# Expert layers on gathered token slots instead of all tokens, with indirect row fetches, in a hybrid attention / mixture-of-experts kernel

## The chip, the cores and the metric

One core of a Trainium2 chip runs one program. It has five engines with queues of their own: TensorE (PE, with its weight loads listed apart as PEld), VectorE (DVE), ScalarE (ACT), GpSimd (POOL) and SyncE (SP), which here only starts transfers. Each engine works through its instructions in order and waits on semaphores for the others. The metric is device time in microseconds (us) of one execution, the median of several runs. All data are fp32.

## The reference, cut to what matters

Eight sequences of 512 tokens with 128 channels go through four residual layers, each on the layernormed input: causal attention, a mixture of experts, an RWKV block, and the same mixture of experts again.

```
x = embeddings                                    # [8, 512, 128]
x = x + attn(layernorm(x))                        # one head of 128 channels
x = x + ffn(layernorm(x))
x = x + rwkv(layernorm(x))                        # itself residual, with a scan over the tokens
x = x + ffn(layernorm(x))

ffn(x):  scores = softmax(x @ Wg)                 # 32 experts
         weights, indices = top_k(scores, 4)
         y[t] = sum over the 4 chosen e of weight * ((silu(x[t] @ W1[e]) * (x[t] @ W3[e])) @ W2[e])
         # hidden size 64; an expert takes at most 2048 of the 4096 tokens
         return y + (silu(x @ Ws1) * (x @ Ws3)) @ Ws2    # shared expert, hidden size 128
```

A token uses 4 of 32 experts, so of a sequence's 512 tokens an expert gets 64 on average.

## The kernel before

The tokens of one sequence are held as four tiles of 128 (token-major: 128 tokens on the partitions) or turned by TensorE into channel-major tiles of 128 channels by 512 tokens. An fp32 product of 128x128 weights with 512 columns shows in the profile as two MATMUL records and two LDWEIGHTS records.

The eight sequences pass through the four layers one behind the other, as a pipeline. Step `s` of the loop at the end of the function `tile_block_kernel` holds attention of sequence `s`, the first expert layer of `s-1`, the RWKV block of `s-2` and the second expert layer of `s-3`; there are 11 steps, and steps 3 to 7 hold all four. Inside a step, `interleave` traces the experts of one layer side by side with attention, and then those of the other layer side by side with RWKV. The tracing order and a scheduler in the language give each engine one fixed order of instructions.

`norm` takes statistics on DVE (L143, L145), the inverse square root on POOL (`rstd`, L146 and L147) and applies it on DVE (L149). `turn` transposes on TensorE (L157).

`route` follows attention and RWKV: scores on TensorE (L173), softmax and the four largest on DVE (L175 to L194), a running count of earlier tokens per expert (POOL, L201, and TensorE, L205 and L206) for the capacity, and the resulting gates, turned, written to DRAM, and read back by `load_gates` with each expert's row spread over 64 partitions (tile `g`, 64 copies).

`experts` works densely: all 16 pairs of experts (two of 64 hidden units fill 128 partitions) on all 512 tokens, plus the shared expert. For each pair: `a` (L251) and `c` (L253) on TensorE, `tanh` on ACT (L257), `h = (tanh + 1) a` on DVE (L258), `v = c * gate` on DVE (L263), `h * v` on POOL (L264), and the product `y` (L239), which accumulates over the pairs in PSUM. At the end `y` is copied (L270), turned and added to the input (L273).

Of the kernel before, what the change touches and what calls it, by code (L numbers as in the profile page):

```python
# [15 lines left out]
P = 128          # partitions, tokens of a tile, channels  # L16
B = 8            # sequences
S = 512          # tokens of a sequence
NJ = S // P      # token tiles of a sequence
E = 32           # experts  # L20
NP = E // 2      # expert pairs: two experts of 64 hidden units fill 128 partitions
NQ = NP // 4     # gate loads of a sequence, each for four pairs
TOPK = 4
CAP = 4 * (B * S * TOPK) // E   # tokens that one expert takes at most
# [3 lines left out]
# Columns of the packed [128, .] weights.  # L28
# [9 lines left out]
# Columns of the packed per-channel vectors.  # L38
# [4 lines left out]
def interleave(heavy, light):  # L43
    """Traces two streams of work side by side: two steps of the light one behind each of the heavy one."""
    for _ in heavy:
        for _ in range(2):
            next(light, None)
    for _ in light:
        pass
# [3 lines left out]
def kernel(ctx: ExitStack, tc: tile.TileContext, x, small, vecs, w13, w2, out):  # L53
    nc = tc.nc

    const = ctx.enter_context(tc.tile_pool(name="const", bufs=1))
    xin = ctx.enter_context(tc.tile_pool(name="xin", bufs=3))
    wk2 = ctx.enter_context(tc.tile_pool(name="wk2", bufs=2))
    wk1 = ctx.enter_context(tc.tile_pool(name="wk1", bufs=1))
    mo = ctx.enter_context(tc.tile_pool(name="mo", bufs=3))  # L60
    gates = ctx.enter_context(tc.tile_pool(name="gates", bufs=2))
    st = ctx.enter_context(tc.tile_pool(name="st", bufs=3))
    dram = ctx.enter_context(tc.tile_pool(name="dram", bufs=2, space=bass.MemoryType.DRAM))
    ps_m = ctx.enter_context(tc.tile_pool(name="ps_m", bufs=2, space=PSUM))
    ps_y = ctx.enter_context(tc.tile_pool(name="ps_y", bufs=1, space=PSUM))
    ps_l = ctx.enter_context(tc.tile_pool(name="ps_l", bufs=3, space=PSUM))

# [1 line left out]
    x0 = {}  # L69

    def load_x(b):
        if b < B:
            x0[b] = xin.tile([P, NJ, P], F32, tag="x0", name=f"x0_{b}")
            nc.sync.dma_start(out=x0[b], in_=x[b].rearrange("(j p) d -> p j d", p=P))

    load_x(0)
    sm = const.tile([P, NCOLS], F32, tag="sm", name="sm")
    cut = _COLS["Wg"][0]
    nc.sync.dma_start(out=sm[:, :cut], in_=small[:, :cut])
    vec = const.tile([P, len(_VECS)], F32, tag="vec", name="vec")  # L80
    nc.scalar.dma_start(out=vec, in_=vecs)
    nc.sync.dma_start(out=sm[:, cut:], in_=small[:, cut:])
    w13s = const.tile([P, NP, 2, P], F32, tag="w13", name="w13s")
    w2s = const.tile([P, NP, P], F32, tag="w2", name="w2s")
    for q in range(NQ):
        nc.sync.dma_start(out=w13s[:, 4 * q : 4 * q + 4], in_=w13[:, 4 * q : 4 * q + 4])
        nc.sync.dma_start(out=w2s[:, 4 * q : 4 * q + 4], in_=w2[:, 4 * q : 4 * q + 4])
    load_x(1)
# [5 lines left out]
    def V(name):  # L94
        i = _VECS.index(name)
        return vec[:, i : i + 1]

# [7 lines left out]
    tri = const.tile([P, P], F32, tag="tri", name="tri")     # tri[i, t] = i <= t  # L105
# [5 lines left out]
    wdec = const.tile([P, 1], F32, tag="wdec", name="wdec")  # -exp(time_decay)  # L111
    nc.scalar.activation(wdec, V("time_decay"), AF.Exp)
    nc.vector.tensor_scalar(wdec, wdec, -1.0, None, ALU.mult)

    # Scores and the values looked for in them, each behind or before four marks that every row
    # has: the match below then finds just the four largest, the first of equals first.
    sc, lst, tot = [], [], []
    for f in range(2):
        s = const.tile([P, NJ, E + 4], F32, tag=f"sc{f}", name=f"sc{f}")
        m = const.tile([P, NJ, 8], F32, tag=f"lst{f}", name=f"lst{f}")  # L120
        for i in range(4):
            nc.gpsimd.memset(s[:, :, E + i : E + i + 1], -1.0 - i)
            nc.gpsimd.memset(m[:, :, 4 + i : 5 + i], -1.0 - i)
        t = wk2.tile([P, NJ + 1, E], F32, tag=f"tot{f}", name=f"tot{f}_start")
        nc.gpsimd.memset(t[:, NJ, :], 0.0)
        sc.append(s)
        lst.append(m)
        tot.append(t)

    def light(name):  # L130
        return ps_l.tile([P, S], F32, tag="l", name=name)

    def flat(t):
        return t.rearrange("p j d -> p (j d)")

# [1 line left out]
    def norm(src, dst, name):  # L137
        """dst = (src - mean) / sqrt(var + eps) over the channels of [128 tokens, 4, 128]."""
        stats = st.tile([P, NJ, 6], F32, tag="stats", name=f"stats_{name}")
        mv = st.tile([P, NJ, 2], F32, tag="mv", name=f"mv_{name}")  # L140
        rstd = st.tile([P, NJ], F32, tag="rstd", name=f"rstd_{name}")
        for j in range(NJ):
            nc.vector.bn_stats(out=stats[:, j, :], in_=src[:, j, :])  # L143
        for j in range(NJ):
            nc.vector.bn_aggr(out=mv[:, j, :], in_=stats[:, j, :])  # L145
        nc.gpsimd.tensor_scalar(rstd, mv[:, :, 1], EPS, None, ALU.add)  # L146
        nc.gpsimd.tensor_tensor(rstd, rstd, nhalf, ALU.pow)  # L147
        for j in range(NJ):
            nc.vector.tensor_scalar(  # L149
                dst[:, j, :], src[:, j, :], mv[:, j, 0:1], rstd[:, j : j + 1], ALU.subtract, ALU.mult  # L150
            )

    def turn(src, name):
        """[128 tokens, 4, 128 channels] -> PSUM [128 channels, 512 tokens], or back."""
        p = light(f"turn_{name}")
        for j in range(NJ):
            nc.tensor.transpose(p[:, j * P : (j + 1) * P], src[:, j * P : (j + 1) * P], ident)  # L157
        return p

    def route(xa, f, b):  # L160
        """Layernorm, scores, the top four experts, capacity; gates go out over the partitions of
        their experts. Gates carry the factor 1/2 of silu(a) = a (1 + tanh(a/2)) / 2."""
# [34 lines left out]
        # tot[j] counts, per place in a tile, the tokens of earlier tiles that chose an expert.  # L197
# [22 lines left out]
        def load_gates(q):  # L220
            """The gates of four pairs, each over the 64 partitions of its expert."""
            t = gates.tile([P, 4, S], F32, tag="g0" if q == 0 else "g", name=f"g_{n}_{q}")
            for h in range(2):
                nc.sync.dma_start(out=t[64 * h : 64 * h + 64], in_=gv[h, q].partition_broadcast(64))
            return t
# [4 lines left out]
    def experts(f, b, xa, put):  # L230
        """xa + the shared expert + the gated experts, all of them on all tokens; put(result)."""
# [9 lines left out]
        for i in range(NP + 1):  # L241
# [8 lines left out]
            a = ps_m.tile([P, S], F32, tag="a", name=f"a_{k}")  # L250
            nc.tensor.matmul(a, wa, xT, start=True, stop=True)  # L251
            c = ps_m.tile([P, S], F32, tag="c", name=f"c_{k}")
# [16 lines left out]
        ys = mo.tile([P, S], F32, tag="ys", name=f"ys_{n}", bufs=2)  # L269
# [63 lines left out]
    def shifted(p, w, bias, name):  # L333
        """Channel-major h from PSUM, behind a column of zeros; and h - (h one token back)."""
        h = wk1.tile([P, S + 1], F32, tag="hT", name=f"hT_{name}")
        nc.gpsimd.memset(h[:, 0:1], 0.0)
        nc.scalar.activation(h[:, 1:], p, AF.Identity, bias=V(bias), scale=V(w))
        d = wk1.tile([P, S], F32, tag="dT", name=f"dT_{name}")
        nc.gpsimd.tensor_tensor(d, h[:, 1:], h[:, :S], ALU.subtract)
        return h, d  # L340

    def mixed(h, d, tm, name):
        """h * tm + (h one token back) * (1 - tm)."""
        t = wk2.tile([P, S], F32, tag="mix", name=f"mix_{tm}_{name}")
        nc.vector.scalar_tensor_tensor(t, d, V(tm), h[:, :S], ALU.mult, ALU.add)  # L345
        return t
# [4 lines left out]
    def rwkv(b):  # L351
# [22 lines left out]
        # pp_t = max(pp_{t-1} + w, k_t); pp, aa and bb start one column early with their initial state.  # L374
# [69 lines left out]
        for c in range(4):  # L444
            p = light(f"kk_{b}_{c}")
            nc.tensor.matmul(p, W("WkeyT", c * P, (c + 1) * P), xk, start=True, stop=True)  # L446
            t = wk1.tile([P, S], F32, tag="kk", name=f"kk_{b}_{c}s", bufs=4)
# [28 lines left out]
    nothing = iter(())  # L476
    for s in range(B + 3):
        a, r = s, s - 2
        m1, m2 = s - 1, s - 3
        interleave(  # L480
            experts(0, m1, x1.pop(m1), lambda t: x2.__setitem__(m1, t)) if 0 <= m1 < B else nothing,
            attention(a) if a < B else nothing,
        )
        interleave(
            experts(1, m2, x3.pop(m2), store(m2)) if 0 <= m2 < B else nothing,
            rwkv(r) if 0 <= r < B else nothing,
        )
# [41 lines left out]
```

## Time and profile before

| | |
|---|---|
| three runs | 1129.38, 1132.04, 1137.63 us; median 1132.04 us |
| profiled execution: span, first to last instruction | 1130.8 us, 9602 instructions |
| mean granted TensorE clock | 0.970 |
| TensorE busy | 988.6 us (87%) |
| DVE busy | 746.7 us (66%) |
| POOL busy | 565.0 us (50%) |
| ACT busy | 311.6 us (28%) |
| moved by DMA | 77.38 MB, of which `g` 128 x 512 KB |

The page gives no other time for the profiled execution than its span; the span lies 1.2 us below the median of the runs, so little lies around it. A row of the table of groups reads: line, engine, operation, output<-input by the program's names, shapes, count, then busy time and the mean of one instruction, then the idle time of that engine just ahead of these instructions and what ended it. "Busy" of TensorE counts overlapped instructions once, so the time that one matmul takes in a stream is read from the distance of starts in the timeline and not from its duration.

### The profile page before, as it was taken

Reading aid. Unit: us, or ns where it says so; the run is one execution under the profiler, and the core shown is the slowest. Engines: PE = TensorE matmul, PEld = TensorE weight load, DVE = VectorE, ACT = ScalarE, POOL = GpSimd, SP = SyncE. Lnnn points to the kernel's source line nnn. Section 1 sums busy time; section 2 is a strip of 40 time slices with the busy share of each in tenths; the row PEclk is TensorE's granted clock in tenths of the full one; section 3 lists DMA queues with packets and bytes.
Section 4 is the critical chain, followed back from the end, with each engine's and each line's share of the span. In section 5 each row is a group of like instructions: output and inputs, shape, how many; then the busy total and the mean of one; then the engine's idle time right before and its main releaser. Section 6 shows DMA issues by size and latency. Waiting matters only on the chain.

```text
span 1130.8 us, 9602 instructions
## 1 busy us (share of the span) xinstructions
PE 988.6 (87%) x2800; PEld 457.6 (40%) x2800; DVE 746.7 (66%) x1809; ACT 311.6 (28%) x578; POOL 565.0 (50%) x613
## 2 busy tenths in 40 slices
PE   4798988799789987998889988899889998888988
PEld 2443543344334433454334543344334443333433
DVE  2456577766866767667776678567685649588543
ACT  2231323223323332232322323232222223231221
POOL 1134345643663457534674347544484547548433
PEclk8799999999999999999999999999999999999999
DMA  5053325105332241133313240331402340142051
GB/s 184 13 118 73 81 50 112 37 13 111 78 73 50 65 96 38 45 79 80 71 38 98 59 101 17 75 86 38 114 26 50 86 112 0 38 96 65 1 123 46
DMA packets 45668, 77.38 MB, mean 68 GB/s; under 512 B 2864, under 2 KB 11184, under 8 KB 45488
## 3 DMA queue, kind: packets, MB, share of 16 engines
q1 hardware_dynamic: 45472, 76.77, 29.1%
q8 instruction: 22, 0.36, 0.1%
q14 instruction: 30, 0.25, 0.1%
q10 hardware_dynamic: 144, 0.01, 0.0%
HBM read 73.62 MB, written 3.15 MB: 68 GB/s over the span
## 4 chain that ended last, share of the span: by engine, by line
PE 47%; DVE 30%; POOL 15%; issue 4%; DMA 2%; ACT 2%; SPq 0%; POOLq 0%; DVEq 0%; ACTq 0%
PE y L239 11%; PE a L251 10%; PE c L253 10%; DVE v L263 5%; POOL h L264 4%; DVE h L258 4%; PE kk L446 3%; PE kv L459 2%; DVE wden L416 2%; PE o L325 2%; PE s L307 2%; DVE xn L149 1%; POOL rstd_f L147 1%; POOL tot L201 1%; DVE sc L184 1%
## 5 line engine op out<-in xcount | busy, mean ns | idle before, releaser
L264 POOL TENSOR_TENSOR h<-h,v 128x512 f32<-128x512 f32 x256 | 336.7, 1316 | 374.4 <-DVE v L263 299.8
L257 ACT ACTIVATE h<-a 128x512 f32<-128x512 f32 x272 | 161.5, 596 | 497.2 <-PE a L251 462.1
L251 PE MATMUL a<-fT,w13s 128*128 128x512 f32 x512 | 270.5, 612 | 11.7 <-DVE h L258 11.4
L239 PE MATMUL y<-h,w2s 128*128 128x512 f32 x512 | 265.0, 604 | 17.5 <-POOL h L264 17.5
L253 PE MATMUL c<-fT,w13s 128*128 128x512 f32 x512 | 269.3, 608 | 5.1 <-DVE v L263 5.1
L258 DVE SCALAR_TENSOR_TENSOR h<-h,a 128x512 f32<-128x512 f32 x272 | 184.7, 679 | 130.5 <-ACT h L257 129.6
L263 DVE TENSOR_TENSOR v<-c,g 128x512 f32<-128x512 f32 x256 | 174.2, 682 | 28.8 <-PE c L253 26.5
L239 PEld LDWEIGHTS y<-h,w2s 128*128 128x128 f32 x512 | 94.7, 195 | 132.0 <-issue 87.4
L253 PEld LDWEIGHTS c<-fT,w13s 128*128 128x128 f32 x512 | 96.7, 196 | 114.0 <-issue 86.9
L251 PEld LDWEIGHTS a<-fT,w13s 128*128 128x128 f32 x512 | 93.4, 196 | 107.6 <-issue 72.3
L146 POOL TENSOR_SCALAR rstd_f<-mv_f 128x4 f32<-128x4 f32 x16 | 3.6, 228 | 78.4 <-DVE mv_f L145 78.4
L149 DVE TENSOR_SCALAR xn<-x,mv_f,rstd_f 128x128 f32<-128x128 f32 x64 | 23.5, 429 | 25.5 <-POOL rstd_f L147 25.5
L446 PE MATMUL kk<-mix_ffn_tmk_c,sm 128*128 128x512 f32 x64 | 29.5, 601 | 4.8 <-DVE mix_ffn_tmk_c L345 4.8
L157 PE MATMUL turn_f<-ident,xn 128*128 128x128 f32 x64 | 16.7, 330 | 18.9 <-DVE xn L149 18.9
L325 PEld LDWEIGHTS o<-vs,prTs 128*128 128x128 f32 x160 | 23.4, 209 | 20.1 <-ACT prTs L320 18.9
L328 DVE SCALAR_TENSOR_TENSOR x<-o,aden,x 128x128 f32<-128x128 f32 x32 | 11.2, 350 | 28.5 <-PE o L325 28.4
L325 PE MATMUL o<-vs,prTs 128*128 128x128 f32 x160 | 27.4, 307 | 2.7 <-ACT prTs L320 2.7
L461 DVE SCALAR_TENSOR_TENSOR num_c<-thr_c,kv 128x512 f32<-128x512 f32 x8 | 5.5, 687 | 34.8 <-PE kv L459 34.8
L416 DVE RECIPROCAL wden<-wden 128x128 f32<-128x128 f32 x32 | 27.9, 913 | 0.0
L314 ACT ACTIVATE pr<-s,abig 128x128 f32<-128x128 f32 (+3 forms) x32 | 16.8, 524 | 36.3 <-DVE abig L311 26.9
L201 POOL TENSOR_TENSOR tot<-tot,chosen 128x32 f32<-128x32 f32 x64 | 16.9, 265 | 16.5 <-DVE chosen L194 13.3
L307 PE MATMUL s<-WKT,WQT 128*128 128x128 f32 (+3 forms) x64 | 25.0, 474 | 0.0
(173 smaller groups left out, 1169.1 us busy)
## 6 DMA issues: line engine op xcount, KB each, us to landing
g<-gd SPq DMA_DIRECT2D x128, 512.0 KB, 6.6
x<-in_x_dram SPq DMA_DIRECT2D x8, 256.0 KB, 4.2
w13s<-in_w_dram SPq DMA_DIRECT2D x4, 512.0 KB, 10.9
out_dram<-xo SPq DMA_DIRECT2D x8, 256.0 KB, 2.2
sm<-in_small_dram SPq DMA_DIRECT2D x1, 1040.0 KB, 7.2
w2s<-in_w_dram SPq DMA_DIRECT2D x4, 256.0 KB, 10.5
gd<-wT SPq DMA_DIRECT2D x16, 64.0 KB, 1.6
sm<-in_small_dram SPq DMA_DIRECT2D x1, 192.0 KB, 3.2
```

The lines of the kernel that those rows point to most:

```text
L149: nc.vector.tensor_scalar(dst[:, j, :], src[:, j, :], mv[:, j, 0:1], rstd[:, j : j + 1], ALU.subtract, ALU.mult)
L239: nc.tensor.matmul(y, w, h, start=(i == 0), stop=(i == NP))
L251: nc.tensor.matmul(a, wa, xT, start=True, stop=True)
L253: nc.tensor.matmul(c, wb, xT, start=True, stop=True)
L257: nc.scalar.activation(h, a, AF.Tanh, scale=0.5)
L258: nc.vector.scalar_tensor_tensor(h, h, 1.0, a, ALU.add, ALU.mult)
L263: nc.vector.tensor_tensor(v, c, g[:, p % 4, :], ALU.mult)
L264: nc.gpsimd.tensor_tensor(h, h, v, ALU.mult)
L307: nc.tensor.matmul(s[:, :n], qT[:, i * P : n], kT[:, :n], start=True, stop=True)
L325: nc.tensor.matmul(o[:, :P], prT[:, j * P : (j + 1) * P], vs[:, j * P : (j + 1) * P], start=(j == 0), stop=(j == i))
L416: nc.vector.reciprocal(den[:, c * P : (c + 1) * P], den[:, c * P : (c + 1) * P])
L446: nc.tensor.matmul(p, W("WkeyT", c * P, (c + 1) * P), xk, start=True, stop=True)
```

## The change

Everything outside the expert layers computes as before. The expert layers get a second form, `route_some` and `experts_some`; the old form is kept as `route_all` and `experts_all` (`a` and `c` in one PSUM pool) and runs again over all sequences behind a branch, if any expert got more tokens than it has slots. `block` builds either form; both are in the program.

- Each expert has 128 slots in a sequence: 28 for each of the four token tiles (`CL`), and 16 shared ones (`CS`) for tokens beyond 28 in a tile. `route_some` finds the slot of each token and expert (`slot`), the four table rows of each token (`rows`, integers) and its four gates (`gate`). The gates no longer go through DRAM.
- `experts_some` builds 0/1 matrices by comparing `slot` with the slot numbers (`one`, 896 columns, and `few`, 512 columns, for each tile), and TensorE gathers the tokens with them: two products of 448 columns and one of 512 for each tile. ACT copies the gathered tokens to `xg`.
- Each expert is multiplied alone on its 128 slots: 64 `a` and `c` products of 64 output rows, and 32 `y` products with 64 rows of contraction, in four groups of eight experts for each sequence and layer; ACT copies the 8 x 128 output columns (`ysb`) and SP writes them to a DRAM table `yd`, 512 KB for each group.
- Each token fetches its four rows with 16 indirect transfers of POOL for each sequence and layer (128 rows of 512 bytes each), and DVE adds them, times the gate. Behind each transfer the text has a `memset` of a tile that nothing reads (`spare`).
- `weave` traces all four streams of a step round-robin, one piece each, instead of `interleave` twice.
- Buffers: `xin` 2 instead of 3, `mo` 2 instead of 3, `ps_m` 3 of one kind instead of 2 + 2, `ps_y` 2 instead of 1; the four `kk` tiles share tiles of other names.
- At the end the fullest slot decides the branch: `over` is loaded into a register of every engine.

In outline:

```
-            y ... for i in range(NP + 1): a, c (512 columns), tanh, h, v, h*v, down()
+def route_some(xa, f, b):                       # from `chosen` on
+        nc.tensor.matmul(cum, tri, flat(chosen), start=True, stop=True)
+        nc.tensor.matmul(cnt, ones, flat(chosen), start=True, stop=True)
+        yield
+        ...                                     # base, q, key, slot on [128, 4 x 32]; all DVE but one POOL add
+        for j in range(NJ):
+            nc.vector.max(out=mk[:, j, :], in_=key[:, j, :])
+        nc.vector.tensor_scalar(rows, mk[:, :, :TOPK], -1.0, None, ALU.add)
+        yield
+        nc.vector.tensor_tensor(eq, key..., mk..., ALU.is_equal)              # 128 x 512
+        nc.gpsimd.tensor_tensor(eq, eq, s..., ALU.mult)
+        nc.vector.tensor_reduce(gate, eq, AX.X, ALU.add)
+def experts_some(f, b, xa, put):
+        for j in range(NJ):
+            for t, lo, c in ((one, 0, CL), (few, CL, CS)):
+                nc.vector.tensor_tensor(t, slot[:, j, :]..., slots[:, lo : lo + c]..., ALU.is_equal)
+            yield
+            for h in range(2):
+                p = mid(f"xg_{n}_{j}_{h}")[:, : E // 2 * CL]
+                nc.tensor.matmul(p, xn[:, j, :], flat(one[:, E // 2 * h : E // 2 * (h + 1), :]), ...)
+                nc.scalar.copy(xg[...], p...)
+            nc.tensor.matmul(left, xn[:, j, :], flat(few), start=(j == 0), stop=(j == NJ - 1))
+            yield
+        nc.scalar.copy(xg[:, :, NJ * CL :], left...)
+        yield
+        yd = dram.tile([P, E, P], F32, tag="yd", name=f"yd_{n}")
+        for g in range(NP // 4):
+            ac = [mid(f"{w}_{n}_{g}") for w in "ac"]
+            for w in range(2):
+                for i in range(4):
+                    for two in range(2):
+                        p = 4 * g + i
+                        nc.tensor.matmul(ac[w][64 * two : 64 * two + 64, i * NS : (i + 1) * NS],
+                            w13s[:, p, w, 64 * two : 64 * two + 64], xg[:, 2 * p + two, :], start=True, stop=True)
+            ...                                 # tanh (ACT), h = (tanh + 1) a, h = 0.5 h c (DVE, 128 x 512)
+            yield
+            ys = [ps_y.tile([P, 4, P], F32, tag="y", ...) for two in range(2)]
+            for i in range(4):
+                for two in range(2):
+                    nc.tensor.matmul(ys[two][:, i, :], h[64 * two : 64 * two + 64, i * NS : (i + 1) * NS],
+                        w2s[64 * two : 64 * two + 64, 4 * g + i, :], start=True, stop=True)
+            ysb = mo.tile([P, 8, P], F32, tag="ysb", name=f"ysb_{n}_{g}")
+            for two in range(2):
+                nc.scalar.copy(ysb[:, two::2, :], ys[two])
+            nc.sync.dma_start(out=yd[:, 8 * g : 8 * g + 8, :], in_=ysb)
+            yield
+        ...                                     # shared expert, token-major: xo = z + xa
+        table = yd.rearrange("s e d -> (s e) d")
+        for j in range(NJ):
+            r = mo.tile([P, TOPK, P], F32, tag="r", name=f"r_{n}_{j}", bufs=3)
+            for k in range(TOPK):
+                nc.gpsimd.indirect_dma_start(out=r[:, k, :], out_offset=None, in_=table,
+                    in_offset=bass.IndirectOffsetOnAxis(ap=rows[:, j, k : k + 1], axis=0))
+                nc.gpsimd.memset(spare, 0.0)
+            yield
+            for k in range(TOPK):
+                nc.vector.scalar_tensor_tensor(xo[:, j, :], r[:, k, :], gate[:, j, k : k + 1], xo[:, j, :],
+                    ALU.mult, ALU.add)
+            yield
+        put(xo)
...
+    again = nc.values_load(over, min_val=0, max_val=1, ...)
+    with tc.If(again > 0), ExitStack() as inner:
+        block(inner, some=False, ...)
```

## The prediction

> **What bounds the kernel now.** I read the page's engine totals first, then the groups by line, then the timelines of ACT, TensorE, DVE and POOL. From the page (busy us and share of the span):
>
> ```profile
> PE 988.6 (87%) x2800; PEld 457.6 (40%) x2800; DVE 746.7 (66%) x1809; ACT 311.6 (28%) x578; POOL 565.0 (50%) x613
> ...
> L264 POOL TENSOR_TENSOR h<-h,v 128x512 f32<-128x512 f32 x256 | 336.7, 1316 | 374.4 <-DVE v L263 299.8
> L251 PE MATMUL a<-fT,w13s 128*128 128x512 f32 x512 | 270.5, 612 | 11.7 <-DVE h L258 11.4
> L239 PE MATMUL y<-h,w2s 128*128 128x512 f32 x512 | 265.0, 604 | 17.5 <-POOL h L264 17.5
> L253 PE MATMUL c<-fT,w13s 128*128 128x512 f32 x512 | 269.3, 608 | 5.1 <-DVE v L263 5.1
> L258 DVE SCALAR_TENSOR_TENSOR h<-h,a 128x512 f32<-128x512 f32 x272 | 184.7, 679 | 130.5 <-ACT h L257 129.6
> L263 DVE TENSOR_TENSOR v<-c,g 128x512 f32<-128x512 f32 x256 | 174.2, 682 | 28.8 <-PE c L253 26.5
> ```
>
> TensorE is the full engine: `a`, `c` and `y` alone keep it busy for 805 us and hardly wait. DVE and POOL trail it. The timeline of ACT gives the pace of the pipeline, by the copy that opens an RWKV block (start us first):
>
> ```profile
> 410.75 0.78 ACT L337 ACTIVATE hT_r<-turn_r,vec 128x512 f32<-128x512 f32 x1 [1.19 <-PE turn_r L157]
> ...
> 545.38 0.78 ACT L337 ACTIVATE hT_r<-turn_r,vec 128x512 f32<-128x512 f32 x1 [1.19 <-PE turn_r L157]
> ...
> 678.79 0.78 ACT L337 ACTIVATE hT_r<-turn_r,vec 128x512 f32<-128x512 f32 x1 [1.19 <-PE turn_r L157]
> ```
>
> A full step takes 133.5 us. That number is what the change has to beat. The timeline of TensorE, in two places, gives the price of a matmul by the distance of starts:
>
> ```profile
> 512.27 1.16 PE L325 MATMUL o<-vs,prTs 128*128 128x128 f32 x8
> 513.26 1.02 PE L253 MATMUL c<-fT,w13s 128*128 128x512 f32 x2
> 514.12 1.02 PE L239 MATMUL y<-h,w2s 128*128 128x512 f32 x2
> ...
> 1066.92 1.06 PE L173 MATMUL lg<-sm,fT 128*128 128x32 f32 x8
> 1067.81 1.10 PE L253 MATMUL c<-fT,w13s 128*128 128x512 f32 x2
> ```
>
> 512 columns take 0.86 us, 128 columns 0.99 / 4 = 0.25 us (I use 0.24), and 32 columns still 0.89 / 4 = 0.22 us: with 128 columns of weights to load for each, a short matmul has a floor of 0.22 us. The same reading on DVE gives 0.60 us for 512 elements (two neighbours below), and the third line, the view of line 184 (min/median/max in ns), a warning:
>
> ```profile
> 1060.57 0.68 DVE L258 SCALAR_TENSOR_TENSOR h<-h,a 128x512 f32<-128x512 f32 x1
> 1061.17 0.87 DVE L143 BATCH_NORM_STATS2 stats_f<-x 128x6 f32<-128x128 f32 x4
> ...
> L184 DVE TENSOR_TENSOR sc<-ex,den x16: 284/1034/1378, 46.9 to 1070.1; 128x128 f32<-128x128 f32 x16
> ```
>
> An operation of 0.28 us with both inputs in SBUF takes a median 1.03 us beside POOL's 1.3 us products. The new work has many of that kind.
>
> **The change, engine by engine.** TensorE loses 256 x 3 x 0.86 = 660 us (and 14 us of transposes). It gains 128 gathers of 448 columns (0.75 us) and 64 of 512, 151 us; 1024 products with 64 output rows at p each; 512 `y` products with 64 rows of contraction, 0.24 each, 123 us. No row has 64 output columns of weights. If two neighbours in different halves of the array run side by side, p is 0.12; if not, 0.24 like `o`. I take 0.18, 184 us, and keep 123 to 246 for the range. So TensorE gets some 215 us lighter: 674 - 151 - 184 - 123 = 216.
>
> The Trainium skill's page "TensorE: Matmul & The Clock Gate", section "Part 3: Packing small matmuls", says that matmuls in different tiles of the array overlap; by it p would be 0.12 and my sum 61 us lower. No row here shows it, and the 0.22 us floor of `lg` is the row against it.
>
> DVE loses 256 x 2 x 0.60 = 307 us of `h` and `v`. It gains 64 x (1.00 + 0.60) = 102 us for `one` and `few` (896 elements: 0.60 + 384 / 0.96 GHz from the 512-element slope), two more 0.60 us operations in 64 groups (77), 256 row additions near `aden`'s 0.35 us less overlap, 0.27 (69), and 16 x 4.6 = 74 for slots, keys and `eq`: about the same load as before. POOL loses 337 us of products and 20 of `tot`, and gains 256 indirect transfers at G each. ACT gains 256 copies of 448 to 512 columns at 0.52 to 0.59 and loses 192 `tanh` at 0.60; it stays far from full.
>
> G is the largest unknown: the trace has no transfer issued by POOL. The nearest row is POOL's `rstd` power (L147, 1.04 us for 4 elements a partition), software working through a short list; I take 1.1. Below lies a POOL memset (L122, 0.105); above, the slowest product (`ev`, L404, 2.11). Those ends move the total by 256 x (G - 1.1), from -255 to +259; near the row I keep 0.7 to 1.6.
>
> The skill's page "DMA: Bandwidth & Descriptors", section "Anatomy of one DMA", gives about 2.0 us plus bytes/436e3 for a transfer issued from GpSimd, 2.15 us for 64 KB, and under "Rules for kernel authors" says that transfers below 64 KB pay mostly overhead: a rule against this change. No row here shows it. If POOL were held that long each time, the sum would be 269 us higher; I expect the transfers to overlap and only the issue to count.
>
> The `spare` memsets, 0.23 us each by the slope of L122 to L125 (0.105 for 4 elements, 0.124 for 32), pace nothing: in the built instruction order all 256 stand before POOL's first transfer, 84 between attention 0's `rstd` and the next, 118 before the second route. 84 x 0.23 = 20 us lies beside attention 0 (`rstd` at 5 and at 38 us in the trace), 118 x 0.23 = 28 us beside the first experts. At double the price the first transfer would come some 20 us later.
>
> **Where it lies: a step in a row.** The built order decides more than the loads. POOL has the 32 transfers of both expert layers in one block, with the `kk` squares between them and the second route's `rstd` behind them. Behind that `rstd` queue, on DVE, the route, all but one of the `one` and `few`, and the RWKV scans; behind the last `few`, on TensorE, the first `a`; behind the last `y`, the table write; behind that, the next 32 transfers. So the parts of a step follow one another:
>
> (1) From the route's `rstd` to the first `a`, DVE: `xn` 1.1, route 3.2, slots and gates 4.6, the last additions 1.6, three norms of 0.87 + 0.36 + 1.11 (7.0), `one` and `few` 12.8, RWKV up to `z` 14.8 (three mixes 2.0, `pp` 1.15, `aa` 2.2, `bb` 1.2, four reciprocals 3.6, the rest 4.7), two attention tiles 2.3: 47; hops to PE, ACT and POOL 5 more; TensorE starts 5 before DVE's end. 47.
>
> (2) To the last `y` of the first layer, TensorE: 128 x 0.18 = 23, 56 x 0.24 = 13.4, attention and `wo` 5.2, and three waits of `y` for two ACT copies (2 x 0.59 + 0.2), 4. 46 (38 to 54 for p).
>
> (3) Copies and table write: 1.2 + 3.5 (between 2.2 us for `out`'s 256 KB and 6.6 for `g`'s 512 KB) + 0.3. 5.
>
> (4) POOL: 32 x 1.1 = 35.2, `dT` and four squares 5.2, `key`, `eq` and `rstd` 2.9. 43.3. DVE's additions, some 25 us of work, lie beside it.
>
> The period is 47 + 46 + 5 + 43.3 = 141.3 us against 133.5.
>
> **The sum.** Up to the second route of sequence 0: `x2` of sequence 0 comes at about 116 us (before: `ys` at 116), then one RWKV and one expert layer (40 + 23 + 5), 16 transfers and 8 us of `kk` and `rstd`: 116 + 68 + 25.6 = 210. Then six periods, the last without attention (-8): 840. Step 9, one layer and RWKV: 40 + 23 + 5 + 25.6 = 94. Step 10: route 15, `one` and `few` 8, groups 22, write 5, transfers 17.6, landing and store 5: 72. Register load and branch 3. 210 + 840 + 94 + 72 + 3 = 1219 us, against the span of 1130.8; the median of the runs lies 1.2 us above that span. I predict 1220.
>
> The branch is not taken: counted from the reference's inputs, an expert needs at most 12 of its 16 shared slots.
>
> **Rivals.**
>
> *Cheap issue and paired products.* TensorE's saving then shows. For it: nothing else in part 4 needs POOL for long, and each 0.1 us of G is 25.6 us. At G = 0.7 and p = 0.12: 1219 - 102 - 61 = 1056 us. It decides the sign from G = 0.77 with p = 0.18, or G = 1.0 with p = 0.12. Against it: POOL's rows with any software in them start at 1.04. Chance 0.21.
>
> *Dear transfers.* DVE's additions have both inputs in SBUF and hold each other and POOL up, as L184 was held. At G = 1.8: 1219 + 179 = 1398 us. Chance 0.15.
>
> *The parts overlap after all.* If the additions and the route let the next `one` and `few` go ahead during part 4, some 20 us of each period vanish: 1219 - 120 = 1099. For it: `one` of the first layer stands ahead of the last additions. Against it: the next seven stand behind the route. Chance 0.08.
>
> *The branch is taken* and the dense form runs behind it: 1219 + 1131 = 2350. Chance 0.01.
>
> The forecast, G near 1.1 and parts in a row, keeps 0.55. Of it about 0.04 fall to faster and 0.05 within 1% (a tie at 1132 needs all terms 7% lower). Measurements of this kernel tell about 1% from no change.
>
> **How the numbers follow.** Likeliest 1220. Faster: 0.18 of the first rival, 0.06 of the third, 0.04 of the forecast's own spread, 0.28. Same: 0.07. Slower: 0.65. The range: G from 0.7 to 1.6 is -102 to +128, p is +-61; the two together, as independent, -119 and +142; with a few more us for hops that I did not see, 1080 to 1380. It holds the middle of the third rival; below it lies the outer half of the first (0.1), above it most of the second (0.1).
>
> **What would show it.** Right: a period near 141 us in the copies of `hT_r`; POOL nearly full in 32 transfers for some 40 us of each step while TensorE has little; TensorE's busy share near 60%. Transfers issued less than 0.8 us apart, or a period below 133, would make the forecast wrong; so would `a` and `c` products 0.12 us apart, by 61 us; a period of 141 with other parts would make the number right for the wrong reason.

## The result and the profile after

The changed kernel takes 1184.8 us (four runs, 1182.6 to 1187.3) where the kernel before takes 1131.9 on the same chip: a ratio of 1.0455, with a 95% interval of 1.0416 to 1.0494. It is slower, as forecast; the forecast of 1220 us was 35 us too high. The branch is not taken. The profiled execution has a span of 1182.9 us at a mean granted TensorE clock of 0.788, where before had 0.970.

From the page of the changed kernel: engine totals, two rows of the slices (tenths of busy time of POOL, tenths of the granted clock), the shares of the chain that ended last, and three groups:

```profile
PE 775.5 (66%) x4689; PEld 480.5 (41%) x4689; DVE 735.3 (62%) x2052; ACT 320.6 (27%) x626; POOL 573.8 (49%) x824
...
POOL 7787427340762328431683407633384417644405
PEclk8595887599866997589965997679965897579595
...
PE 28%; DVE 26%; POOL 26%; issue 11%; DMA 5%; ACT 4%; POOLq 0%; DVEq 0%; ACTq 0%
...
L367 POOL DMA_INDIRECT r<-yd,rows x256 | 251.0, 980 | 102.1 <-issue 65.3
...
L374 DVE SCALAR_TENSOR_TENSOR xo<-r,gate,xo 128x128 f32<-128x128 f32 x256 | 104.1, 412 | 85.2 <-DMA r<-yd,rows 83.2
...
L371 POOL MEMSET spare<- 128x192 f32 x256 | 66.5, 260 | 14.3
```

The same two rows, clock and chain, from the page of the kernel before:

```profile
PEclk8799999999999999999999999999999999999999
...
PE 47%; DVE 30%; POOL 15%; issue 4%; DMA 2%; ACT 2%; SPq 0%; POOLq 0%; DVEq 0%; ACTq 0%
```

TensorE fell from 988.6 to 775.5 us, DVE kept its load, and no engine is above 66%; yet the kernel is slower. The chain says why: it goes over TensorE, DVE and POOL in nearly equal shares, where before TensorE had almost half, so the engines now work one after the other. The POOL row of the slices shows the beat, some 6 to 8 tenths and then 4 or less. The row under it beats too: TensorE's granted clock falls to 5 to 7 tenths in every step.

The pace, read as before from ACT's copies that open an RWKV block (start and duration in us):

```profile
374.41 0.78 ACT L558 ACTIVATE hT_r<-turn_r,vec 128x512 f32<-128x512 f32 x1 [1.34 <-PE turn_r L209]
510.87 0.78 ACT L558 ACTIVATE hT_r<-turn_r,vec 128x512 f32<-128x512 f32 x1 [1.34 <-PE turn_r L209]
647.31 0.78 ACT L558 ACTIVATE hT_r<-turn_r,vec 128x512 f32<-128x512 f32 x1 [1.34 <-PE turn_r L209]
```

A full step takes 136.5 us, against 133.4 to 134.6 before and 141.3 forecast.

One step in four windows, beginning with the transfers, the forecast's part 4; the next two are roughly its part 1 and its parts 2 and 3, and the last is part 4 of the next step (window, length, then busy us and instructions of PE, PEld, DVE, ACT, POOL, then granted clock, DMA share, GB/s):

```profile
574.00:622.00 48.00, 21.70 (x64) 11.11 (x64) 25.58 (x86) 5.62 (x10) 39.06 (x42) 0.75 0.19 52
622.00:667.00 45.00, 31.35 (x77) 15.97 (x78) 34.52 (x106) 12.23 (x23) 16.41 (x16) 0.69 0.02 7
667.00:712.00 45.00, 41.73 (x446) 31.27 (x444) 28.86 (x68) 21.90 (x45) 9.30 (x11) 1.00 0.23 94
712.00:760.00 48.00, 25.26 (x64) 13.58 (x64) 25.45 (x85) 5.62 (x10) 38.31 (x40) 0.70 0.16 44
```

POOL leads while the rows are fetched, then DVE in the routes and the 0/1 matrices, then TensorE in the products, and POOL again. Only in TensorE's own window is the clock at 1.00.

The price of one transfer, from the timeline of POOL:

```profile
576.70 0.95 POOL L367 DMA_INDIRECT r<-yd,rows  x1 [0.30 <-issue]
577.95 0.95 POOL L367 DMA_INDIRECT r<-yd,rows  x1 [0.31 <-issue]
579.20 0.95 POOL L367 DMA_INDIRECT r<-yd,rows  x1 [0.30 <-issue]
```

Each holds POOL for 0.95 us, and another 0.30 us pass before the next: 1.25 us from start to start. The price of the small products, from the timeline of TensorE, by the distance of starts (16 records are eight products):

```profile
675.18 1.09 PE L326 MATMUL a<-xg,w13s 128*64 128x128 f32 x16
676.10 1.04 PE L326 MATMUL c<-xg,w13s 128*64 128x128 f32 x16
676.98 0.60 PE L326 MATMUL a<-xg,w13s 128*64 128x128 f32 x6
...
704.61 1.16 PE L338 MATMUL y<-w2s,h 64*128 64x128 f32 x16
705.71 1.16 PE L546 MATMUL o<-vs,prTs 128*128 128x128 f32 x8
```

The two groups of `a` and `c` take 1.80 us, 0.113 for each product; `y` takes 1.10 / 8 = 0.14.

### The profile page after: what moved, and what is told of

Same layout as the page of the kernel before. It is cut to its first block, busy times and chain, and to the rows that moved or that the text cites. A ratio compares the mean times of both kernels' runs of the same rounds, so it can differ in the third digit from the quotient of the medians.

```text
span 1182.9 us, 13848 instructions
## 1 busy us (share of the span) xinstructions
PE 775.5 (66%) x4689; PEld 480.5 (41%) x4689; DVE 735.3 (62%) x2052; ACT 320.6 (27%) x626; POOL 573.8 (49%) x824
## 4 chain that ended last, share of the span: by engine, by line
PE 28%; DVE 26%; POOL 26%; issue 11%; DMA 5%; ACT 4%; POOLq 0%; DVEq 0%; ACTq 0%
POOL r L367 13%; PE y L338 5%; PE a L326 5%; PE c L326 4%; POOL spare L371 3%; DMA r<-yd,rows 3%; DVE one L303 3%; DVE xo L374 3%; DVE few L303 3%; PE xg L310 2%; DMA yd<-ysb 2%; PE o L546 2%; PE left L314 2%; PE s L528 1%; PE lg L225 1%
## 5 line engine op out<-in xcount | busy, mean ns | idle before, releaser
L367 POOL DMA_INDIRECT r<-yd,rows x256 | 251.0, 980 | 102.1 <-issue 65.3
L310 PE MATMUL xg<-one,xn 128*128 128x448 f32 x256 | 138.2, 659 | 52.3 <-DVE one L303 46.3
L374 DVE SCALAR_TENSOR_TENSOR xo<-r,gate,xo 128x128 f32<-128x128 f32 x256 | 104.1, 412 | 85.2 <-DMA r<-yd,rows 83.2
L314 PE MATMUL left<-few,xn 128*128 128x512 f32 x128 | 81.3, 723 | 18.5 <-DVE few L303 18.4
L332 DVE SCALAR_TENSOR_TENSOR h<-h,a 128x512 f32<-128x512 f32 x64 | 43.9, 686 | 76.3 <-ACT h L331 75.9
L326 PE MATMUL a<-xg,w13s 128*64 128x128 f32 x1024 | 84.1, 286 | 5.8 <-ACT xg L316 5.8
L338 PE MATMUL y<-w2s,h 64*128 64x128 f32 x1024 | 83.3, 290 | 1.1 <-DVE h L333 0.5
L326 PE MATMUL c<-xg,w13s 128*64 128x128 f32 x1024 | 78.2, 281 | 2.2 <-DVE h L332 2.2
L303 DVE TENSOR_TENSOR one<-slot,slots 128x896 f32<-128x896 f32 x64 | 76.7, 1199 | 0.0
L331 ACT ACTIVATE h<-a 128x512 f32<-128x512 f32 x64 | 38.5, 601 | 54.4 <-PE a L326 53.1
```

The lines of the kernel that those rows point to most:

```text
L303: nc.vector.tensor_tensor(t, slot[:, j, :].unsqueeze(2).to_broadcast([P, E, c]), slots[:, lo : lo + c].unsqueeze(1).to_broadcast([P, E, c] ...
L310: nc.tensor.matmul(p, xn[:, j, :], flat(one[:, E // 2 * h : E // 2 * (h + 1), :]), start=True, stop=True)
L314: nc.tensor.matmul(left, xn[:, j, :], flat(few), start=(j == 0), stop=(j == NJ - 1))
L326: nc.tensor.matmul(ac[w][64 * two : 64 * two + 64, i * NS : (i + 1) * NS], w13s[:, p, w, 64 * two : 64 * two + 64], xg[:, 2 * p + two, :], ...
L332: nc.vector.scalar_tensor_tensor(h, h, 1.0, ac[0], ALU.add, ALU.mult)
L338: nc.tensor.matmul(ys[two][:, i, :], h[64 * two : 64 * two + 64, i * NS : (i + 1) * NS], w2s[64 * two : 64 * two + 64, 4 * g + i, :], star ...
```

## The experiments

Each kernel ran beside the kernel before on its chip; the intervals are 95% intervals of the ratio to it. "The changed kernel" is at 1184.8 us.

**1. A quarter of the transfers** (`one_row`):

```
-            for k in range(TOPK):
+            for k in range(1):
                 nc.gpsimd.indirect_dma_start(...)
...
-                    xo[:, j, :], r[:, k, :], gate[:, j, k : k + 1], ...
+                    xo[:, j, :], r[:, 0, :], gate[:, j, k : k + 1], ...
```

> Each tile of 128 tokens fetches one row per token instead of four: 64 transfers instead of 256, and 64 memsets of `spare`; the four additions stay, but all read the first fetched row, so three of each token's four rows are left out of the computation. Theory (the transfers stand in a row in every step, because `e` and `kk` of the next step are queued behind them on POOL, and the next step's work stands behind these): 192 transfers of 0.95 us and 0.30 us of gap are taken out, 192 x 1.25 = 240 us, so about 945 us, and the distance of the hT_r copies falls from 136.5 to about 106 us. Rival (the transfers are hidden, the step is set by VectorE and TensorE, which keep all their work): 1170 to 1185 us. Between the two, some 1030 us, if another engine takes over the bound once the transfers are short.

1024.8 us, ratio 0.905 (0.901 to 0.908): 160 us less than the changed kernel, and a step of 119.4. So the transfers stand in the path, but only two thirds of their 240 us come back, and a few of these are the 192 memsets of `spare` that went with them (all 256 are worth 7.5 us, experiment 3). Part 4, from the first transfer to the next route's `rstd`, now takes 28.2 us where it took 47.4, 19 us less for 30 us of transfers. Its window (columns as above) shows where the rest stays:

```profile
515.90:544.10 28.20, 16.90 (x60) 9.34 (x60) 25.63 (x85) 4.55 (x8) 15.08 (x16) 0.87 0.08 28
```

DVE is busy for 25.6 of the 28.2 us. The same 25 us of work lay beside 47 us of POOL before, and now they are nearly the whole part. The third expectation, "some 1030 us, if another engine takes over the bound", was the right one.

**2. Neighbouring products in the same half of the array** (`no_pairs`):

```
-                for i in range(4):
-                    for two in range(2):
+                for two in range(2):
+                    for i in range(4):                  # a and c; the same for y
```

> The order of the 64-row products is changed so that neighbours lie in the same half of the array; same products, same number. Theory (neighbours in different halves run beside each other, which is why a product took 0.115 us in `a`/`c` and 0.137 us in `y`): without it each takes about 0.24 us; 1024 `a`/`c` products x 0.125 + 512 `y` x 0.10 = up to 180 us of TensorE time, 128 + 53; all of it stands in the part of the step in which TensorE works through the experts, so 1290 to 1360 us. Rival (the distance of the small products is what the sequencer gives, whichever half they are in): 1180 to 1190 us, and the products keep 0.115 and 0.137 us.

1223.8 us, ratio 1.081 (1.076 to 1.086): 39 us more. From its timeline of TensorE:

```profile
705.06 1.71 PE L338 MATMUL y<-w2s,h 64*128 64x128 f32 x16
706.70 1.25 PE L326 MATMUL a<-xg,w13s 128*64 128x128 f32 x13
...
709.20 0.91 PE L528 MATMUL s<-WKT,WQT 128*128 128x384 f32 x2
```

`y` now takes 1.64 / 8 = 0.205 us each, and 16 products of `a` and `c` take 2.50 us, 0.156 each on average; around the change from `a` to `c`, where the half changes too, their records still alternate (left out above), so some of these still ran in pairs. So pairing is real, but in this order a product costs 0.156 to 0.205 us, not the 0.24 that I expected, and the loss is little more than a third of the least that I gave (105 us).

**3. No memsets of `spare`** (`no_spare`):

```
-                nc.gpsimd.memset(spare, 0.0)
```

> The 256 memsets of `spare` and the tile are left out. Theory (they are all issued early, 84 beside the first attention block, and 118 in the 37 us ahead of the first fetch, where they hold the first fetch back by a few us): 5 to 10 us less, 1175 to 1180 us; the distance of the hT_r copies stays at 136.5 us. Rival (the prediction's: hidden wholly): 1182 to 1188 us. Third (the memsets hold the transfers apart and without them the transfers are queued worse): slower than 1190 us.

1177.3 us (1175.7 to 1178.0), ratio 1.040 (1.037 to 1.043): 7.5 us less. The first transfer starts at 92.0 us instead of 99.0, and the step stays at 137. The memsets cost what they hold back the start of the pipeline, and nothing later.

**4. More work for TensorE while it idles** (`warm`):

```
                 nc.gpsimd.memset(spare, 0.0)
+            warm = light(f"warm_{n}_{j}")
+            for _ in range(2):
+                nc.tensor.matmul(warm, ident, sm[:, :S], start=True, stop=True)
             yield
```

> The changed kernel with two matmuls of 512 columns on constants ahead of each tile's additions, whose product is read by nobody: 128 matmuls of 0.86 us at full clock, 14 us of TensorE in each step, all in the part in which the 32 transfers are issued and TensorE was busy for 25 of 48 us at a mean granted clock of 0.70. Theory A (the low clock costs time: matmuls there take up to twice as long, and busier it would not fall): the clock of that part and of the next rises above 0.8, and the added work is paid back: 1165 to 1190 us. Theory B (the clock falls for another reason, or the matmuls there are off the path): the clock stays at 0.70 and the time is 1185 to 1210 us. Were all 128 in the path and the clock unchanged: 1185 + 110 to 220 us.

1204.9 us, ratio 1.064 (1.061 to 1.067). The mean clock rises from 0.788 to 0.844, in two windows of the fetch from 0.75 and 0.70 to 0.81 and 0.85. One group of the changed kernel, and the same one with the added products:

```profile
L667 PE MATMUL kk<-mix_ffn_tmk_c,sm 128*128 128x512 f32 x64 | 50.0, 933 | 19.1 <-DVE mix_ffn_tmk_c L566 10.0 <-remote 9.1
```

```profile
L670 PE MATMUL kk<-mix_ffn_tmk_c,sm 128*128 128x512 f32 x64 | 33.9, 639 | 0.8 <-DVE xo L360 0.8
```

The mean `kk` record falls from 933 to 639 ns. 110 us of added products cost 20 us: most of them lay in idle time or were paid back by the faster clock, and the run cannot part these two. The added products also take buffers of the PSUM pool `ps_l`, so the 20 us are not their time on TensorE alone. The run lies between the theories: the clock rises with more work, and the products are faster with it, but filling the idle time in this way does not pay.

The Trainium skill, on the page "TensorE: Matmul & The Clock Gate", section "HAM oscillation — how this bites in real kernels", says that gaps in TensorE's work longer than about 3.4 us let a clock gate fall to half rate, so that each burst begins cold. The windows agree in the direction and the depth: 0.69 to 0.75 where TensorE has gaps, 1.00 where it has almost none, and in no stretch of 5 us of the changed kernel below 0.50. How long a gap must be, no run here shows.

**5. The order and the buffers without the gathering** (`dense_woven`, `dense_halves`). The first drops the 128-slot form and the branch:

```
     with ExitStack() as inner:
-        block(inner, some=True, ...)
-    again = nc.values_load(over, ...)
-    with tc.If(again > 0), ExitStack() as inner:
         block(inner, some=False, ...)
...                                              # the loads at the start follow it
```

> The dense form alone, as the changed kernel has it behind its branch: the dense experts of before in the new weave, with the new buffers and without the branch and the 128-slot form. All of the reference is computed. It tells what order and buffers are worth without the gathering. Theory (they are worth little): 1120 to 1160 us. Rival (the dearer period came from the weave, by which the four streams wait for each other): over 1180 us. Third (the weave by itself is an improvement that the 128-slot form then gives away): under 1110 us.

The second also goes back to two weaves a step, `weave((experts(0, ...), 1), (attention(a), 2))` and then `weave((experts(1, ...), 1), (rwkv(r), 2))`:

> The dense form alone in the new buffers, in the order of before (two weaves a step). With the four streams woven at once it took 1222 us, the kernel before takes 1132. Theory (the order costs the 90 us): 1125 to 1150 us. Rival (the smaller buffers cost them: two instead of three of `x0` and of the experts' tiles): 1200 to 1230 us.

1222.0 us, ratio 1.079 (1.076 to 1.082), and 1152.0 us, ratio 1.018 (1.013 to 1.022). Weaving four streams at once costs the dense form 70 us; what else differs from the kernel before, the buffers among it, costs 20. Under the same weave the 128-slot form is 37 us *faster* than the dense one (1184.8 against 1222.0). The changed kernel with the two weaves (`two_halves`) is the fourth corner:

> The changed kernel with the order of before: a step is two weaves one behind the other, first the first layer's experts with the attention, then the second layer's experts with the recurrence, with two rounds of the lighter stream to one of the experts, where the changed kernel weaves all four at once. The rest, the memsets of `spare` too, is kept; all of the reference is computed. Theory (woven together, the two layers end together and their 32 transfers stand in one row in which no other engine has much to do): in two halves the 16 transfers of one layer lie beside the products of the other; the step falls from 136.5 to 105 to 120 us and the time to 980 to 1080 us. Rival (POOL's transfers still hold up what the next half needs, the parts only come in another order): 1150 to 1200 us.

1176.9 us, ratio 1.040 (1.036 to 1.044), steps of 128 to 136 us. The theory falls: the order that is worth 70 us to the dense form is worth 8 to the gathered one.

**6. The fetch taken out of the row.** In `late_fetch` the transfers and additions are a generator of their own, woven one step later than the products that fill its table:

```
-        a, m1, r, m2 = s, s - 1, s - 2, s - 3
+        m1, g1, r, m2, g2 = s - 1, s - 2, s - 3, s - 4, s - 5
         ...
+            work.append((fetch_some(0, g1, put2(g1)), 1))
+            work.append((fetch_some(1, g2, store(g2)), 1))
```

> The fetch (32 transfers and additions of a step) is a stage of its own, woven one step later than the experts that write its table; `yd` has a buffer per layer, `xo` of the first layer three, the memsets of `spare` are left out; 13 steps instead of 11. All of the reference is computed. Theory (the four parts of a step stand in a row only because the transfers need the last `y` of the same step and the next step's POOL work is queued behind them): the transfers go beside the products of the next experts, and the step falls from 136.5 us to what the busiest engine has in it, VectorE with about 92 us, POOL with about 70: 95 to 110 us a step, 930 to 1020 us in all. Rival (the parts stand in a row for another reason, such as VectorE's own order, or POOL's transfers now hold `e` and `kk` back in the middle of the step): a step of 125 us or more, over 1130 us with the two extra steps.

1165.5 us, ratio 1.030 (1.026 to 1.034). The theory falls in this form: full steps with both fetches still take 134 to 136 us. In `spread_fetch` the text issues one transfer in every second round:

> As the run with the late fetch (13 steps, the fetch a stage of its own, no memsets of `spare`), but a fetch stream now issues one transfer in every second round of the weave instead of four in one round, over all 36 rounds of a step, and the additions of a tile come some rounds after its last transfer. All of the reference is computed. In the run with the late fetch a step of two fetches still took 136 us, with its 32 transfers in a row on POOL (614 to 664 us) and `rstd_a`, `rstd_p`, `rstd_r` behind them. Theory (the step is long because POOL's queue holds the other streams behind 32 transfers in a row, wherever that row stands): spread, the step falls to 95 to 115 us, towards the 92 us that VectorE has in it, and the time to 950 to 1080 us. Rival (each step is a chain through the recurrence and the attention that is near 130 us long whatever POOL does): 1120 to 1170 us, the step still above 128 us. The run with one row of four, 119 us a step, speaks for something between: 105 to 120 us and 1010 to 1100 us if VectorE or TensorE's low clock takes over.

1166.4 us, ratio 1.029 (1.026 to 1.032), and its trace shows that the edit did not reach the queue: the scheduler had put the transfers together again, 32 of them from 617 to 666 us, the next norm behind the last:

```profile
664.01 0.99 POOL L382 DMA_INDIRECT r<-yd,rows  x1 [0.16 <-issue]
665.30 0.94 POOL L382 DMA_INDIRECT r<-yd,rows  x1 [0.30 <-issue]
666.28 0.25 POOL L197 TENSOR_SCALAR rstd_f<-mv_f 128x4 f32<-128x4 f32 x1
```

In `spread_queue` POOL keeps the order of the text:

```
+            with tc.manual_schedule(engines={mybir.EngineType.Pool}):
                 weave(*work)
```

> The same code as the run with the spread fetch, but POOL issues its instructions in the order in which the code emits them, where so far the scheduler put the 32 transfers of a step in a row again (616 to 665 us). Now one or two POOL operations of the other streams lie between two transfers over the whole step. All of the reference is computed. Theory (the row of 32 transfers on POOL, with `rstd_f`, `rstd_a`, `rstd_p` and `rstd_r` behind it, makes the step 136 us long): a step of 95 to 115 us, towards VectorE's 92 us, and 950 to 1080 us. Rival (the step is a chain of its own through attention, recurrence and experts): 1120 to 1170 us. Third (fixed order makes POOL wait for VectorE and with it all engines for each other): over 1200 us.

1123.9 us, ratio 0.9927 (0.9903 to 0.9952): 42.5 us less than the same code in the scheduler's order, in full steps of 124 and 128 us where that has 135 and 134. POOL now does both in turn:

```profile
658.69 1.84 POOL L382 DMA_INDIRECT r<-yd,rows  x1 [0.16 <-issue]
660.55 1.27 POOL L633 TENSOR_TENSOR ww<-ww,qq 128x512 f32<-128x512 f32 x1
661.98 1.71 POOL L382 DMA_INDIRECT r<-yd,rows  x1 [0.16 <-issue]
```

So giving up the row of 32 was worth 6 to 11 us a step, where I had expected 20 to 40; the edit fixes the order of everything else on POOL too, and the run cannot part the two. Why not more? Windows of one of its steps:

```profile
548.00:578.00 30.00, 27.91 (x351) 23.17 (x351) 18.09 (x42) 13.55 (x28) 4.04 (x4) 1.00 0.29 111
578.00:622.00 44.00, 28.62 (x107) 16.75 (x103) 30.41 (x104) 9.54 (x17) 25.97 (x28) 0.79 0.13 42
622.00:645.00 23.00, 9.36 (x25) 5.37 (x25) 16.96 (x74) 2.49 (x5) 12.53 (x15) 0.59 0.10 30
645.00:674.00 29.00, 22.40 (x62) 10.30 (x61) 26.46 (x37) 13.45 (x27) 23.54 (x22) 0.96 0.08 23
```

The parts still follow one another: in TensorE's 30 us POOL has four instructions. The waits of POOL in that kernel name the one that stands in front of its queue (us in total, times, longest), and the page's chain by line shows what became of the transfers:

```profile
POOL xs L669 <- DVE xq L667: 140.5, 8, 25.8
...
POOL r L382 13%; DMA r<-yd,rows 6%; PE y L337 4%; PE a L325 4%; PE c L325 3%; DVE one L302 2%; DVE xo L372 2%; DVE few L302 2%; PE xg L309 2%; PE s L543 2%; PE left L313 2%; PE o L561 2%; POOL e L624 1%; POOL eq L285 1%; POOL rstd_f L198 1%
```

The RWKV sum `xs` waits for DVE's `xq`, up to 25.8 us in a step, and the transfers that could go beside the products stand behind it. And the transfers did not leave the chain: they hold 13% of it, as in that of the changed kernel, and now stand between the POOL operations of the recurrence, such as `ww` above. That these two hold the step at 126 us is argued from the trace; a kernel without either was not tried.

**7. Both orders.** `halves_late` has two weaves a step, the first layer's fetch in the second half of the same step and the second layer's in the first half of the next, 12 steps, POOL in the order of the text; `halves_free` is the same with the scheduler's order.

> Two weaves a step as in the run with two halves, POOL in the order of emission as in the run with the spread queue. The fetch is a stage of its own: the first layer's 16 transfers stand in the second half of the same step, beside the recurrence and the second layer's products; the second layer's in the first half of the next step, beside attention and the first layer's products; one transfer in a round, beginning four rounds late. So the pipeline is one step longer than that of the changed kernel and one shorter than that of the spread fetch; no memsets of `spare`. All of the reference is computed. Theory (what was won by spreading, 136.5 to about 126 us a step, holds in halves too, and each half has one route, one set of `one` and `few` and one set of products, so that VectorE's and TensorE's parts of the two layers can lie beside each other): 105 to 118 us a step, 1000 to 1080 us. Rival (the halves follow one another on POOL's fixed queue and each is a chain of some 63 us): 126 us a step or more, 1110 to 1180 us.

> The same code with POOL's order left to the scheduler, which puts a layer's 16 transfers in blocks of four to twelve. If the fixed queue holds the halves apart, this is the faster one: 1020 to 1100 us. If blocks of transfers ahead of `rstd_a`, `rstd_p` and `rstd_r` are what costs, it is slower than the one with the fixed queue by 10 to 50 us, and near the 1177 us of the run with two halves.

1135.8 us, ratio 1.003 (1.000 to 1.005), steps of 131 us: the rival. And 1123.1 us, ratio 0.9931 (0.9904 to 0.9958), steps of 127: faster than with the fixed queue, though not into the range that I gave for that case. Here, with a layer's 16 transfers mostly in blocks of 12 and 4 and the halves apart, the scheduler's order is the better one. `spread_queue` and `halves_free` are the two versions with the whole computation that come out below the kernel before, by 0.7%.

## Why the prediction was right, and where it was not

**Parts of a step in a row: right, and the reason for the sign.** The chain is shared by three engines, and the four windows show them one after the other; the rival that the parts overlap after all did not come. The forecast's marks came: TensorE 66% busy (60 named), POOL at 39 of 48 us in part 4, a step above 133. One of its marks of being wrong came too, `a` and `c` products 0.12 us apart, which it had priced at 61 us. Experiment 1 shows that the transfers are in the path, and experiment 6 that the order of POOL's queue is a part of it.

**The sum, against the trace** (cut at POOL's `rstd_f` of the second route, at 216.3, 1024.4 and 1109.8 us):

| | predicted | measured |
|---|---|---|
| up to the second route of sequence 0 | 210 | 216.3 |
| six periods | 840 | 808.1 |
| step 9 | 94 | 85.4 |
| step 10, branch, end | 75 | 73.1 |

What the forecast had too much is mostly in the periods, and there the terms err in both directions. One step, from 621.3 us (the start of `rstd`; with 138.9 us it is one of the longer ones):

| part | predicted | measured |
|---|---|---|
| (1) `rstd` to the first `a`, DVE | 47 | 53.9 |
| (2) to the last `y` of the first layer, TensorE | 46 | 30.5 |
| (3) to the first transfer | 5 | 7.2 |
| (4) transfers, to the next `rstd` | 43.3 | 47.4 |

That the sum came within 2% of this step is luck in part: part 2 was 15.5 us too long, and the other three together were 13 too short.

**Part 2 was half as long again as measured, by p and by `y`.** I took 0.18 us for a product of `a` or `c` and 0.24 for `y`. They take 0.113 and 0.14: 128 x 0.113 + 56 x 0.14 is 22 us instead of 36, and with the 9 us of attention and waits that I had added this is 31, the measured part. The Trainium skill's page "TensorE: Matmul & The Clock Gate", section "Part 3: Packing small matmuls", had it right with its overlap of products in different tiles of the array; I had weighed it against a floor that I read from `lg`, whose products use all rows, and met it halfway. Experiment 2 shows the floor to be the wrong row: even unpaired, a half-size product takes 0.156 to 0.205 us. For `y` I had not applied the rule at all.

**Part 1 was too short, by waits.** The step's part 1 as a window (columns as above), DVE's longest wait in it, and `one` and `few` from DVE's timeline, with a POOL product between:

```profile
621.33:675.18 53.85, 37.35 (x93) 18.30 (x94) 43.26 (x117) 16.28 (x33) 21.24 (x22) 0.74 0.02 5
...
DVE bb L623 <- ACT ks L617: 3.5, 1, 3.5
...
654.99 1.08 DVE L303 TENSOR_TENSOR one<-slot,slots 128x896 f32<-128x896 f32 x1
655.99 0.68 DVE L303 TENSOR_TENSOR few<-slot,slots 128x512 f32<-128x512 f32 x1
...
663.91 2.24 POOL L625 TENSOR_TENSOR ev<-ks,v 128x512 f32<-128x512 f32 x1 [1.38 <-ACT ks L617]
...
665.18 1.91 DVE L303 TENSOR_TENSOR one<-slot,slots 128x896 f32<-128x896 f32 x1
```

DVE is busy for 43.3 us, where I had 42 (its 47 less the 5 by which TensorE starts earlier), so the work was priced well. It waits for 10.6 us, where I had allowed 5 for hops. `one` and `few` take the 1.00 and 0.60 us that I had, from start to start, where nothing disturbs them; three of the 15 in this part stand beside POOL's long products and take 1.4 to 1.9 us. The prediction's row of line 184 had warned of that; over the whole run, such cases included, the means of their records are 1.20 and 0.85 us.

**Part 3 was 2 us too short.** The chain shows 5.05 us for the last write of the table, where I had 3.5, and 0.9 us from there to the first transfer, where I had 0.3.

**Part 4: G was 1.25, not 1.1.** 32 x 0.15 = 4.8 us, and the part is 4.1 longer than forecast. The gap of 0.30 us that the profile calls "issue" belongs to the price; I had none in the trace of before. POOL is not held for the 2.15 us a transfer that the prediction named against its sum. Neither rival on G came: at 1.25 transfers are not dear, and cheap issue with paired products came true in its second half alone, 61 us by the prediction's own price, while G took 38 of them back.

**The memsets: wrong by 7.5 us.** "Hidden", I said, beside the first experts. They take 0.26 us each, where I had 0.23, and one starts every 0.32 us in the 37 us of them before the first fetch, where I had 28; without them the first transfer starts 7 us earlier.

**What no step of it held: the clock.** I priced TensorE's products at the clock of before. A lighter TensorE that waits for DVE and POOL is granted 0.69 to 0.75 in parts 1 and 4, and `kk` shows it with its mean of 933 ns, where before it had 601. TensorE's "lighter by 216 us" came out as 213 by busy time, though the small products alone were 1024 x 0.067 + 512 x 0.10 = 120 us cheaper than priced; that the low clock filled the difference is argued, not shown, and the busy time of overlapped products need not fall as their distance does. How many us of the step the clock costs stays open: experiment 4 raised it and paid for it in the same run.

**What the forecast did not ask: what the order alone does.** It took the woven order as given and counted its parts. Experiment 5 shows that the order is the larger loss (90 us with the buffers) and the gathering a gain (37 us) under it; but the corners don't add up, since the gathered form hardly gains from the old order (8 us), and in that order it is 25 us slower than the dense one (1176.9 against 1152.0). So it would be wrong to put the slower result down to the order alone or to the gathering alone.

## What to carry to other kernels

When a change takes work from the fullest engine and gives the others serial work, count the step as a chain of parts and price each part on the engine that leads in it; the shares of the page will look like a gain. A burst of transfers issued by POOL had its issue time in the chain here wherever it stood in the queue, so look at what is queued behind it, and look in the trace, not in the text, for the order that was built. Taking one suspect out of a chain returns its length only down to the next engine's work in the same part: 160 of 240 us here.

## What the runs showed of the hardware

- An indirect transfer of 128 rows of 512 bytes occupies POOL for 0.95 us and is followed by 0.30 us of "issue"; with DVE and other POOL work in between, single ones took 1.3 to 2.6 us and the mean rose from 0.98 to 1.10 us (`spread_queue`).
- Products of 64 output columns or 64 contraction rows, fp32, 128 columns: 0.113 and 0.14 us when neighbours lie in different halves of the array, 0.156 and 0.205 with four of one half in a row. In `no_pairs` records of `c` start between the last ones of `a` (698.46 `c`, 698.56 `a`, 698.62 `c`), though the text has all eight `a` first.
- The granted clock of one core falls to 0.50 in some stretches where TensorE is a quarter to a half busy: between 620 and 640 us of `spread_queue`, with 2.6 and 4.9 us busy in the two tens of microseconds. The share alone does not set it: in the ten before, with 3.9 us busy, it was still 0.85.
